# The rank of what feeds TensorE's small products, in a list scheduler's backward pass

## Chip, cores, metric

The kernel runs on one core of one Trainium2 chip. The metric is device time in microseconds (us) of one execution, as a median of several runs; lower is better.

## What is computed

64 samples `x` of 64 channels by 1024 steps go through a per-sample channel mixing (a 64x64 matrix picked by a condition index) and then, for each of the 4096 rows, a feed-forward layer of 1024 to 1024 with a gated low-rank part (8 experts of rank 16, two of them chosen per row). The input is added at the end:

```python
y = einsum('bct,bcd->bdt', x, weights[condition])
logits = einsum('bsd,ed->bse', y, gate_w)             # 8 experts
w, sel = top_k(logits, 2); w = softmax(w)
w_full = sum(one_hot(sel, 8) * w[..., None], axis=2)
low = einsum('bsd,erd->ebsr', y, lora_A)
out = einsum('bsd,od->bso', y, base_w) + base_b
out = out + 2.0 * einsum('ebsr,eor,bse->bso', low, lora_B, w_full)
return x + out
```

All of it is float32.

## The kernel before

**Tiling.** The 4096 rows are 32 tiles of 128 (two samples each). Mixing channels and multiplying by the weights commute, so the kernel first forms z = x times the weights (1160 columns in three chunks: the low-rank and gate columns with the first part of the output, then two chunks of 388), and mixes the channels afterwards by a product with a 128x128 block-diagonal condition matrix. The contraction of 1024 is cut into four blocks `k` of 256, each of two halves of 128.

**Three products for one.** Every float32 operand is split into a high and a low part: ScalarE casts the high part (`copy`, recorded at L232), VectorE subtracts for the low part (`sub`, recorded at L229), and TensorE adds up high times high, low weights times high, and high weights times low. One `zstep` (line 402) is these three matmuls for one half (`f`) of one block.

**Stages.** Tiles 0 to 3 are multiplied plainly (the list `PLAIN`, 96 steps of two halves), because the weights are still arriving: `load_w` brings a weight block b(k+1)(c+1), `split_w` splits it, `load_x` and `split_x` do the same for x blocks. From tile 4 on, two tiles at a time form a pair that is multiplied with a fast 2x2-block scheme of fewer products (`p1` to `p20`), on sums of x blocks (`sum_x`, L290) and sums of weight blocks (`mix_w`, L340), with results put together by ScalarE and VectorE (L710, L727).

**Small products.** For every tile, z is split again (`split_z`) and multiplied with the condition matrix (`sums`, line 428). For chunk 0 this gives the gate's logits; `gate` chooses and weighs the experts in small steps on ScalarE and VectorE, `tr` transposes the weighted low-rank part on TensorE, and `sums` with `with_lora` adds its product. These products (`sums` and `tr`) are short next to the stream of z products. `add` is called with `first=True` for them in tiles 0 to 29. `finish` closes a chunk, `store` writes the tile.

**The condition matrix** of a tile comes by `load_cond` (line 386): GpSimd issues an indirect gather into `bdr`, ScalarE casts it to `bdh` (L392's first `add`, recorded at L232), VectorE subtracts to `bdl` (L229). There are two buffers of each, so tiles 0 and 2 share one. The gather is a step with `early=True`.

**The order of the work** is made by a planner. The kernel's functions don't emit instructions; they call `add` on a `Program`, which records a step: its engine (or engines), a cost, what it reads and writes, a due time, and some marks. `run` (line 109) then does two passes:

- a backward pass gives each step a rank `late`: the latest start by which everything that depends on it is still in time, by the steps' costs, the time `hop` for a signal between engines, and `lag` for a transfer;
- a forward pass simulates the engines with these costs. For the engine that is free first, it takes among the steps that are ready the one with the smallest `(not first, late)`, and emits it. A step is ready when all that it depends on has ended, by the planner's own costs; a step with `early` is moreover not offered before `late - AHEAD` (10 us); a `first` step is offered MARGIN (1.2 us) after its inputs are ready, and then goes ahead of all steps that are not `first`.

The emitted order is the order of each engine's queue. Every engine works through its queue in that order, and an instruction whose input hasn't arrived holds up those behind it. The z products have the extra key `"order"`, so among themselves they keep the written order. Planner costs that matter here: ScalarE's `START` 0.74, GpSimd's 1.7, `FLIGHT` 2.0 and 1/360e3 us per byte for a transfer.

SP issues the loads of x (L274), weights (L324), tokens (L375) and `in_lb` (L589); GpSimd issues the gathers (L389), the accumulating loads (L376, L383) and the stores (L458). Eight semaphores are used in turn for SP's transfers, so a transfer also waits for the one eight places before it to land.

Of the kernel before, what the change touches and what calls it, by code (L numbers as in the profile page):

```python
# [52 lines left out]
MARGIN = 1.2  # L53
# [24 lines left out]
class Program:  # L78
# [30 lines left out]
    def run(self):  # L109
        steps, n = self.steps, len(self.steps)  # L110
        succ = [[] for _ in steps]
        for i, s in enumerate(steps):
            for d in s["deps"]:
                succ[d].append(i)
        hop = lambda a, b: SAME[a] if a == b else HOP[a]
        late = [0.0] * n
        for i in reversed(range(n)):
            s = steps[i]
            c, e = min(s["eng"].values()), next(iter(s["eng"]))
            late[i] = min([s["due"] - c] + [late[j] - hop(e, next(iter(steps[j]["eng"]))) - s["lag"] - c  # L120
                                            for j in succ[i]])
        left = [len(s["deps"]) for s in steps]
        ready, end, by = [0.0] * n, [0.0] * n, [None] * n
        free = dict(START)
        cand = {e: set() for e in HOP}

        def offer(i):
            for e in steps[i]["eng"]:
                t = max([steps[i]["after"]] + [end[d] + hop(by[d], e) for d in steps[i]["deps"]])
                if steps[i]["early"]:  # L130
                    t = max(t, late[i] - AHEAD)
                t += MARGIN if steps[i]["first"] else 0.0
                cand[e].add((i, t))

        for i in range(n):
            if not left[i]:
                offer(i)
        done, port, wire = 0, 0.0, 0.0
        while done < n:
            best = None  # L140
            for e, c in cand.items():
                if c:
                    t = max(free[e], min(max(r, port) if steps[i]["port"] else r for i, r in c))
                    if best is None or t < best[0]:
                        best = (t, e)
            t, e = best
            i, r = min(((i, r) for i, r in cand[e] if (max(r, port) if steps[i]["port"] else r) <= t + 1e-9),
                       key=lambda q: (not steps[q[0]]["first"], late[q[0]], q[0]))
            for f in steps[i]["eng"]:
                cand[f] = {q for q in cand[f] if q[0] != i}  # L150
            end[i], by[i] = t + steps[i]["eng"][e], e
            free[e] = end[i]
            if steps[i]["size"]:
                end[i] = wire = max(end[i] + FLIGHT, wire) + steps[i]["size"] * DMA
            if steps[i]["port"]:
                port = end[i]
            steps[i]["fn"](e)
            done += 1
            for j in succ[i]:
                left[j] -= 1  # L160
                if not left[j]:
                    offer(j)
        return max(end)
# [686 lines left out]
```

## Time and profile before

| | |
|---|---|
| median of 3 runs | 460.23 us (459.87 to 460.57) |
| the profiled execution | 460.46 us, of which span 458.7 us |
| granted TensorE clock | 1.00 of full speed over the span |
| bytes from and to HBM | 57.74 MB read, 16.78 MB written |

The profile is of one execution. Its span goes from the first to the last instruction; the execution's own time holds some 1.8 us more around it. PE is TensorE's matmuls and PEld its weight loads, DVE is VectorE, ACT ScalarE, POOL GpSimd, SP the engine that issues most loads. Lines are those of the kernel's file; since ScalarE's casts and VectorE's subtractions go through helpers, they all carry L232 and L229, and are told apart by the names of their tiles (out<-in). In a timeline a row has its start and duration in us, then engine, line, operation, tiles and shapes; the brackets at its end give the time that the engine stood idle just before it, and what ended that. The ends of matmuls are modelled: back to back they start 0.176 us apart and are shown as 0.34 long.

### The profile page before, as it was taken

How to read it: one execution, taken by the hardware profiler on the slowest of the kernel's cores; microseconds unless marked ns; L12 is line 12 of the kernel's file. 1: busy time of each engine (PE TensorE's matmuls, PEld its weight loads, DVE VectorE, ACT ScalarE, POOL GpSimd, SP SyncE). 2: the span in 40 equal slices, each digit the busy share in tenths (PEclk: the TensorE clock that was granted, in tenths of full speed). 3: DMA queues.
4: the chain of work that ended last, by engine and by line, in shares of the span. 5: the costliest groups of instructions: out<-in, count | busy, mean ns of one | idle time of the engine just before them, and what ended most of it. 6: DMA issues, size and time to landing. Idle time of an engine off the chain costs nothing.

```text
span 458.7 us, 7562 instructions
## 1 busy us (share of the span) xinstructions
PE 452.3 (99%) x2615; PEld 449.0 (98%) x2615; DVE 383.4 (84%) x940; ACT 227.5 (50%) x520; POOL 88.8 (19%) x107
## 2 busy tenths in 40 slices
PE   8999999999999999999999999999999999999995
PEld 8999999999999999999999999999999999999995
DVE  5999997878989788796997979789797988888674
ACT  5864656543636345373543646355354544546231
POOL 3010215121303021120303003030120403103000
PEclk9999999999999999999999999999999999999999
DMA  8942739976778462764846566573655746456142
GB/s 284 336 126 42 160 98 205 214 215 198 176 211 202 172 161 88 215 128 167 188 137 189 119 185 150 172 181 110 196 120 177 182 128 195 114 176 148 48 137 91
DMA packets 36085, 75.00 MB, mean 164 GB/s; under 512 B 4416, under 2 KB 22096, under 8 KB 36048
## 3 DMA queue, kind: packets, MB, share of 16 engines
q0 software_dynamic: 10560, 36.72, 33.7%
q1 hardware_dynamic: 25200, 37.41, 26.0%
q10 hardware_dynamic: 288, 0.40, 0.3%
q8 instruction: 20, 0.33, 0.3%
q14 instruction: 17, 0.14, 0.1%
HBM read 57.74 MB, written 16.78 MB: 162 GB/s over the span
## 4 chain that ended last, share of the span: by engine, by line
PE 93%; DMA 5%; DVE 1%; SPq 1%; ACT 0%; issue 0%; ACTq 0%
PE ps_z L409 71%; PE ps_o L441 15%; PE ps_a L441 6%; DMA xtok<-in_lb 2%; DMA w_b<-in_w 2%; DMA xr<-in_xT 1%; PE ps_a L492 1%; SPq L324 0%; SPq L274 0%; DVE xtok L451 0%; DVE wl_b_b L229 0%; ACT wh_b_b L232 0%; DVE st L727 0%; ACTq L232 0%
## 5 line engine op out<-in xcount | busy, mean ns | idle before, releaser
L229 DVE TENSOR_TENSOR xl<-xr,xh 128x512 fp32r<-128x512 f32 (+1 forms) x138 | 92.3, 672 | 20.6 <-ACT xh L232 20.3
L409 PE MATMUL ps_z<-wh_t_p,xh 128*128 128x388 f32 (+1 forms) x308 | 105.3, 342 | 0.1
L409 PE MATMUL ps_z<-wl_t_p,xh 128*128 128x388 f32 (+1 forms) x308 | 104.3, 339 | 0.0
L409 PE MATMUL ps_z<-wh_t_p,xl 128*128 128x388 f32 (+1 forms) x308 | 104.3, 339 | 0.0
L232 ACT CAST xh<-xr 128x512 fp32r<-128x512 f32 (+1 forms) x136 | 82.5, 610 | 37.4 <-PE ps_z L409 32.8
L727 DVE TENSOR_TENSOR st<-ps_z,st 128x388 f32<-128x388 f32 x126 | 70.3, 559 | 21.0 <-PE ps_z L409 19.9
L290 DVE TENSOR_TENSOR xr<-xr 128x256 f32<-128x256 f32 (+1 forms) x139 | 69.7, 528 | 3.1 <-DMA xr<-in_xT 2.7
L409 PE MATMUL ps_z<-wh_b_p,xh 128*128 128x388 f32 (+1 forms) x180 | 61.4, 341 | 0.0
L409 PE MATMUL ps_z<-wh_b_p,xl 128*128 128x388 f32 (+1 forms) x180 | 60.8, 338 | 0.0
L409 PE MATMUL ps_z<-wl_b_p,xh 128*128 128x388 f32 (+1 forms) x180 | 60.8, 338 | 0.0
L409 PEld LDWEIGHTS ps_z<-wh_t_p,xh 128*128 128x128 f32 x308 | 57.8, 188 | 1.2 <-DVE st L727 0.7
L409 PEld LDWEIGHTS ps_z<-wl_t_p,xh 128*128 128x128 f32 x308 | 57.9, 188 | 0.0
L409 PEld LDWEIGHTS ps_z<-wh_t_p,xl 128*128 128x128 f32 x308 | 57.8, 188 | 0.0
L458 POOL DMA_DIRECT2D out<-xtok x30 | 16.8, 560 | 193.5 <-DVE xtok L451 92.2
L232 ACT CAST zh<-st 128x388 fp32r<-128x388 f32 (+1 forms) x70 | 36.2, 517 | 24.2 <-DVE st L727 17.0
L376 POOL DMA_DIRECT2D xtok<-in_bias x28 | 27.4, 980 | 97.3 <-DMA xtok<-in_x 90.0
L389 POOL DMA_INDIRECT bdr<-in_cw,rows x32 | 36.1, 1129 | 28.0 <-DVE zl L229 16.6
L710 ACT ACTIVATE ps_z<-ps_z 128x388 f32<-128x388 f32 x42 | 20.1, 478 | 41.1 <-PE ps_z L409 39.0
L451 DVE TENSOR_TENSOR xtok<-ps_o,xtok 128x388 f32<-128x388 f32 x56 | 31.0, 559 | 11.0 <-PE ps_o L441 10.6
L229 DVE TENSOR_TENSOR zl<-st,zh 128x388 fp32r<-128x388 f32 (+1 forms) x70 | 38.9, 556 | 1.5 <-ACT zh L232 1.2
L409 PEld LDWEIGHTS ps_z<-wh_b_p,xh 128*128 128x128 f32 x180 | 33.8, 188 | 0.2
L409 PEld LDWEIGHTS ps_z<-wl_b_p,xh 128*128 128x128 f32 x180 | 33.8, 188 | 0.0
(130 smaller groups left out, 871.1 us busy)
## 6 DMA issues: line engine op xcount, KB each, us to landing
xr<-in_xT SPq DMA_DIRECT2D x128, 128.0 KB, 3.1
xtok<-in_bias POOLq DMA_DIRECT2D x32, 512.0 KB, 7.2
out<-xtok POOLq DMA_DIRECT2D x30, 512.0 KB, 3.1
xtok<-in_x SPq DMA_DIRECT2D x28, 512.0 KB, 3.7
w_b<-in_w SPq DMA_DIRECT2D x10, 388.0 KB, 5.8
xtok<-in_x POOLq DMA_DIRECT2D x4, 512.0 KB, 6.2
out<-xtok SPq DMA_DIRECT2D x4, 194.0 KB, 2.5
bdr<-in_cw,rows POOLq DMA_INDIRECT x32, 5.3
```

The lines of the kernel that those rows point to most:

```text
L229: eng[e].tensor_tensor(o, a, b.bitcast(F32), ALU.subtract)
L232: (nc.scalar.copy if e == ACT else nc.vector.tensor_copy)(o, a)
L290: add(DVE, tt_cost(2 * P * len(os)), lambda e: nc.vector.tensor_tensor(some(xr, os), some(xr, xs), some(xr, ys), f), [("xr", u) for u in s ...
L376: add(POOL, 1.1, lambda e: nc.gpsimd.dma_start(xtok[j], bias.broadcast_to([P, T]), accum_op=ALU.add), writes=keys, size=TWICE * 4.0 * T * P)
L389: add(POOL, 1.04, lambda e: nc.gpsimd.indirect_dma_start(out=bdr[j], out_offset=None, in_=cw, in_offset=bass.IndirectOffsetOnAxis(ap=rows[ ...
L409: nc.tensor.matmul(z, l[:, j, n], w.ap()[:, f, :cols], start=(start and q == 0), stop=(stop and q == 2), skip_group_check=True)
L441: nc.tensor.matmul(d, l, r, start=(start and m == 0), stop=(stop and m == len(mms) - 1), skip_group_check=True)
L451: add(DVE, 0.09 + 0.00104 * (s.stop - s.start), lambda e: nc.vector.tensor_tensor(xtok[j][:, o], bank[b][:, s], xtok[j][:, o], ALU.add), [ ...
L458: add(POOL, 1.0, lambda e: nc.gpsimd.dma_start(out[i * P:(i + 1) * P, o], xtok[j][:, o]), src, size=4.0 * P * (o.stop - o.start))
L492: add(PE, 0.107, lambda e: nc.tensor.matmul(tp, low[i % 2][:, :ER], ident, is_transpose=True, start=False, stop=False, skip_group_check=True),
L710: add(ACT, 0.2 + 0.00085 * W, lambda e: nc.scalar.mul(z[b], z[x], scale), [BANKS[x]], [BANKS[b]])
L727: add(DVE, 0.09 + 0.00104 * W, lambda e: nc.vector.tensor_tensor(unit(u), a(), b(), f), reads, [ukey(u)])
```

## The change

One term is added in the backward pass. Where a step's successor is marked `first`, the successor's rank is taken MARGIN (1.2 us) earlier before the step's own rank is worked out from it. MARGIN is the distance that the forward pass already keeps between the end of a small product's inputs and the time at which it is offered.

```diff
@@ -117,7 +117,7 @@
         for i in reversed(range(n)):
             s = steps[i]
             c, e = min(s["eng"].values()), next(iter(s["eng"]))
-            late[i] = min([s["due"] - c] + [late[j] - hop(e, next(iter(steps[j]["eng"]))) - s["lag"] - c
+            late[i] = min([s["due"] - c] + [late[j] - MARGIN * steps[j]["first"] - hop(e, next(iter(steps[j]["eng"]))) - s["lag"] - c
                                             for j in succ[i]])
         left = [len(s["deps"]) for s in steps]
         ready, end, by = [0.0] * n, [0.0] * n, [None] * n
```

The steps, their costs, their data and their engines stay as they are. Only `late` differs, and with it the choice in the forward pass and the time at which `early` steps are offered.

## The prediction

> **What bounds the kernel now.** I read the page first: its span, its engines, and the stretches of the span.
>
> ```profile
> span 458.7 us, 7562 instructions
> PE 452.3 (99%) x2615; PEld 449.0 (98%) x2615; DVE 383.4 (84%) x940; ACT 227.5 (50%) x520; POOL 88.8 (19%) x107
> ```
>
> TensorE (PE) is idle for 6.4 us in all. The table of busy time by stretch says where (columns: us; PE, PEld, DVE, ACT, POOL busy; clock; DMA share; GB/s):
>
> ```profile
> 0.00:20.00 20.00, 18.67 (x119) 17.78 (x120) 14.91 (x29) 13.31 (x23) 4.08 (x11) 1.00 0.92 328
> 20.00:60.00 40.00, 39.88 (x230) 39.45 (x229) 38.15 (x81) 24.36 (x53) 6.08 (x7) 1.00 0.49 116
> 100.00:430.00 330.00, 330.00 (x1904) 329.00 (x1903) 278.99 (x711) 159.07 (x374) 64.55 (x74) 1.00 0.61 164
> 453.00:459.00 6.00, 0.91 (x6) 0.58 (x4) 1.09 (x2) 0.00 (x0) 0.00 (x0) 0.95 0.35 124
> ```
>
> From 60 us on nothing is left to win: matmul follows matmul at 0.176 us. The change adds and removes no instruction, it only reorders. So it can gain the few stalls in the first 30 us and the last 20, and it can lose wherever a reordered feeder comes late. The place with little lead is the head, where each engine runs just behind the loads. So I read the timeline there, and the view of the tile `bdr` (the gathered condition weights).
>
> ```profile
> 8.21 0.40 ACT L232 CAST xh<-xr 128x256 fp32r<-128x256 f32 x1
> 9.01 0.84 ACT L232 CAST wh_b_b<-w_b 128x776 fp32r<-128x776 f32 x1 [0.40 <-DMA w_b<-in_w]
> 9.76 0.40 ACT L232 CAST xh<-xr 128x256 fp32r<-128x256 f32 x1
> 9.88 0.97 DVE L229 TENSOR_TENSOR wl_b_b<-w_b,wh_b_b 128x776 fp32r<-128x776 f32 x1 [0.24 <-ACT wh_b_b L232]
> 10.77 0.42 DVE L229 TENSOR_TENSOR xl<-xr,xh 128x256 fp32r<-128x256 f32 x1
> 11.33 0.34 PE L409 MATMUL ps_z<-wh_b_b,xh 128*128 128x384 f32 x1
> 11.51 0.34 PE L409 MATMUL ps_z<-wl_b_b,xh 128*128 128x384 f32 x1
> 11.68 0.35 PE L409 MATMUL ps_z<-wh_b_b,xl 128*128 128x384 f32 x1
> ```
>
> The cast at 9.01 is the split of weight block b22, the one at 9.76 the split of x(1,1) (tile 1, k=1). DVE subtracts behind them. The three matmuls are the first step that uses x(1,1); its last one needs `xl`, which ends at 11.19. That is a lead of 0.49 us and no more.
>
> ```profile
> 14.85 0.29 ACT L232 CAST bdh<-bdr 128x128 fp32r<-128x128 f32 x1
> 6.94 1.06 POOL L389 DMA_INDIRECT bdr<-in_cw,rows  x1 [0.18 <-issue]
> DMA to landing us min/median/max: 5.5/5.5/5.5
> ```
>
> The first gather is issued at 6.94 and lands 5.5 us later, at 12.44 (the last line is for that gather alone). Its cast waits for nothing today, because it runs at 14.85.
>
> **What the change moves, part by part.** *Rank.* Line 120 takes MARGIN (1.2) off the rank of whatever feeds a product marked `first` (5 for each of the first 30 tiles, 150 in all), and once more for every such product further down the chain. From the first cast the chain before passes 4 such products, after 20, since the PSUM banks link the tiles. Worked out with the costs in the code, ranks near the start move by 8 to 16, the last ones by 1.2. The gather is a step with `early`, offered no sooner than its rank less AHEAD: its rank goes from 16.23 to 5.34, and so it is offered at once. By the planner's own constants it is issued at 3.4 (1.7 + 1.1 + 0.6) and its cast fits at 8.5, into ScalarE's short wait for b22. So the cast of tile 0 moves from place 18 to place 10 on ScalarE, its subtraction on VectorE from 32 to 11. The built program shows it:
>
> ```
> ACT before: wh_b_b | xh | wh_b_b (b22) | xh | wh_b_p | xh | ... | xh | bdh (waits for the gather)
> ACT after:  wh_b_b | xh | bdh (waits for the gather) | wh_b_b (b22) | xh | wh_b_p | xh | bdh | ...
> ```
>
> *The wait that this adds.* GpSimd's queue and SP's first 19 transfers stand as before, and none of them up to 12.4 us waits for ScalarE, so the gather should land at 12.44 again. Queued behind the waiting cast are b22's split, x(1,1)'s, and every later weight block; VectorE waits for these, PE for both. Worked through:
> 1. Cast start: 12.44 plus 0.02 to 0.10. The upper is the weight block b23 further on (the chain has it landing at 21.51 + 3.63 = 25.14, its cast starts at 25.24); I take 0.10: 12.54.
> 2. The cast takes 0.29, and ScalarE starts the next 0.09 before the end (9.01 + 0.84 against 9.76): b22's split starts at 12.74 instead of 9.01, 3.73 late.
> 3. x(1,1)'s `xl` is late by the same and ends at 14.92. The third matmul had 0.49 of lead, 0.03 of it signalling (9.85 to 9.88). PE is late by 3.73 - 0.46 = 3.27.
>
> PE's hole comes in two pieces. From 11.33 to `xh` of x(1,1) at 10.16 + 3.73 = 13.89, 2.6 us; then two matmuls, then 0.7 for `xl`. Behind it the feeders are fast enough not to open it again: a weight block and an x block cost ScalarE 1.15 (9.01 to 9.76 plus 0.40), VectorE 1.31 at most (9.88 to 10.77 plus 0.42), with a 0.96 weight sum between some of them, and feed four steps of 0.53 = 2.1 us on PE.
>
> *What goes away.* The only other stall worth naming before the tail:
>
> ```profile
> 26.12 0.97 DVE L229 TENSOR_TENSOR wl_b_b<-w_b,wh_b_b 128x776 fp32r<-128x776 f32 x1 [0.56 <-ACT wh_b_b L232]
> 26.67 0.34 PE L409 MATMUL ps_z<-wh_b_b,xh 128*128 128x388 f32 x1
> 27.14 0.44 PE L409 MATMUL ps_z<-wl_b_b,xh 128*128 128x388 f32 x1
> 27.42 0.34 PE L409 MATMUL ps_z<-wh_b_b,xl 128*128 128x388 f32 x1
> ```
>
> b23 landed at 25.14 and its low half came late: 27.14 - 26.67 - 0.176 = 0.29, then 0.10 more, 0.40 in all. After, PE gets here at 29.9, and the load does not move by that much (it waits for a buffer that VectorE frees at about 20.9, and was issued at 21.51). ScalarE takes tile 0's `low` copy before b23's cast; the product it copies (26.15) moves up five steps of 0.53, to 26.8 after the shift, and ends near 27.5; copy 0.27, cast 0.84 and subtraction 0.97 put the low half near 29.6. The 0.40 goes.
>
> *Edits I cost at nothing.* On PE 171 of 820 steps change place, by 10 at most, small products forward. PE has no gap between 60 and 430 that these could fill, so no gain; if a small product came before its feeder, PE would stand for that feeder, 0.56 for a `zl`. That is covered by VectorE's idle 51 us of 330. SP's 52 moved transfers (4 places at most, 0.45 each) are mostly x loads that wait for a buffer anyway. The load of `in_lb` goes behind four x loads of 128 KB, 512 KB or about 1.5 us at 328 GB/s: it lands near 22.5 instead of 21.0, and its cast, now four places later on a late ScalarE, comes after that. GpSimd's 39 moves (3 places at most) put gathers before stores, and only the next token load waits for a store, for its buffer; if that came late, the closing add (0.56) and then PE's bank would be late. The last 30 us have unmarked products (tiles 30 and 31): the same.
>
> Sum against the profiled execution: 458.7 + 3.27 - 0.40 = 461.6 of span; with its own 1.8 around the span (460.46 in all) 463.3. That execution lies 0.23 above the median, so **463.1 us**, 0.6% slower.
>
> A rule that speaks against stopping there is in the Trainium skill, TensorE: Matmul & The Clock Gate, Part 1: a PE idle for one window of about 3.4 us drops to half clock, and needs a busy window to recover. By the page, a drop would add some 1.7 us (an estimate: half of one window). The hole is 2.6 + 0.7 with two matmuls between, just under the page's limit.
>
> The row: the last matmul starts at 453.57, and the clock of 453 to 459 is 0.95, which is 0.6 us at half. So PE stood for 4.6 us before the clock fell. 2.6 is well short of that, so I count no drop.
>
> **Rivals.**
> - *The clock falls in the hole.* For it: the two pieces are close together. The kernel opens with 39 matmuls over 3.94 us to raise the clock; half of such a stretch lost is 2.0: **465.1**. Chance 0.10.
> - *A second wait.* VectorE is late by 3.73, PE by 3.27, and VectorE is busy 38.15 of 40 us from 20 to 60. If b23's 0.40 stays, and the 0.46 of lead lost shows once more: 463.1 + 0.86 = **464.0**. Against it: half of ScalarE and the slots of later weights have us to spare. Chance 0.12.
> - *The gather comes sooner: not slower.* The same view over all 32 gathers reads 2.4, 5.3 and 7.4 us (least, median, most); 2.4 is also the quickest of the first four. It would land at 9.34, b22's split start at 9.64, 0.63 late, PE 0.17 late; less 0.40: 460.23 - 0.23 = **460.0**. It decides below a landing of about 9.6. Against it: DMA at 328 GB/s and a share of 0.92 in that stretch. With it stands the case that the reorder does nothing. Chance 0.06.
>
> **How the numbers follow.** The forecast has 0.72. About 0.2% (0.9 us) is what a measurement of this kernel can tell from no change. Below 461.2 lies only the last rival: same 0.04, faster 0.02 (it would need gains I cannot point at), slower 0.94. Range: a first gather as slow as the slowest, 7.4, adds 1.9 (465.0), as the clock does; a landing 1.1 sooner gives 462.0. So 462.0 to 465.1.
>
> **What would show it.** ScalarE's idle before its first `bdh`, near 3.9 us, put down to the DMA of `bdr`; `bdh` near 12.5; PE's first steps with a gap at 11.3 to 13.9 and a smaller one to 14.9; no gap at b23; from 60 on every chain piece about 2.9 later than before; the same tail. It is wrong if `bdh` stands at 9 to 10, if the stall is regained later, or if the clock row of 12 to 20 is below 1.

## The result, and the profile after

The changed kernel takes 464.86 us (median of 6 runs, 463.44 to 466.23) beside 460.21 (459.87 to 460.69) for the one before: a ratio of 1.0101 with an interval of 1.0088 to 1.0114. It is slower by about 1%, some 4.65 us. The profiled execution took 466.0 us, of which 464.1 are span, so it is one of the slower ones; before's was 460.46 with 458.7 of span. The sums below are between these two spans, 5.4 us apart.

The head of the page and the busy time by stretch (us; PE, PEld, DVE, ACT, POOL busy; clock; DMA share; GB/s), changed kernel:

```profile
span 464.1 us, 7585 instructions
PE 453.9 (98%) x2615; PEld 449.9 (97%) x2615; DVE 384.1 (83%) x940; ACT 227.5 (49%) x520; POOL 90.8 (20%) x107
```

```profile
0.00:20.00 20.00, 14.99 (x88) 13.76 (x89) 10.82 (x24) 10.52 (x21) 5.82 (x12) 0.91 0.92 327
20.00:60.00 40.00, 40.00 (x232) 39.89 (x231) 37.09 (x77) 22.37 (x49) 5.56 (x6) 1.00 0.39 93
100.00:430.00 330.00, 329.95 (x1905) 328.35 (x1904) 280.02 (x711) 159.95 (x374) 64.01 (x73) 1.00 0.60 162
```

PE's busy time in all is 1.6 us more than before with the same 2615 matmuls, and its idle time is larger as well. Both come from the first stretch: 88 matmuls in 20 us where there were 119, at a mean clock of 0.91 where there was 1.00. From 20 us on, the picture is that of before.

ScalarE's timeline, changed kernel:

```profile
8.71 0.40 ACT L232 CAST xh<-xr 128x256 fp32r<-128x256 f32 x1
13.25 0.30 ACT L232 CAST bdh<-bdr 128x128 fp32r<-128x128 f32 x1 [4.14 <-DMA bdr<-in_cw,rows]
13.46 0.83 ACT L232 CAST wh_b_b<-w_b 128x776 fp32r<-128x776 f32 x1
14.20 0.40 ACT L232 CAST xh<-xr 128x256 fp32r<-128x256 f32 x1
```

The cast of the gathered block now stands ahead of b22's split and of x(1,1)'s. ScalarE waits 4.14 us for the gather with both queued behind it; b22's split starts at 13.46, before at 9.01.

TensorE's timeline, changed kernel:

```profile
10.87 0.34 PE L409 MATMUL ps_z<-wh_b_b,xl 128*128 128x384 f32 x1
14.65 0.44 PE L409 MATMUL ps_z<-wh_b_b,xh 128*128 128x384 f32 x1 [3.44 <-ACT xh L232]
14.93 0.33 PE L409 MATMUL ps_z<-wl_b_b,xh 128*128 128x384 f32 x1
15.68 0.69 PE L409 MATMUL ps_z<-wh_b_b,xl 128*128 128x384 f32 x1 [0.41 <-DVE xl L229]
16.16 0.52 PE L409 MATMUL ps_z<-wh_b_b,xh 128*128 128x384 f32 x1
16.48 0.52 PE L409 MATMUL ps_z<-wl_b_b,xh 128*128 128x384 f32 x1
```

The matmul at 15.68 is the one that stood at 11.68 before: 4.00 us late. Behind the hole the next two start 0.32 us apart, not 0.176, and are shown 0.52 long. That is TensorE at half clock.

At b23 the stall has gone (TensorE, changed kernel; before, these three started at 26.67, 27.14 and 27.42):

```profile
29.45 0.34 PE L409 MATMUL ps_z<-wh_b_b,xh 128*128 128x388 f32 x1
29.63 0.34 PE L409 MATMUL ps_z<-wl_b_b,xh 128*128 128x388 f32 x1
29.81 0.34 PE L409 MATMUL ps_z<-wh_b_b,xl 128*128 128x388 f32 x1
```

The balance of the spans, from the distances of matmul starts over 0.176 us in the two traces: +4.00 at the hole, +1.46 from the half clock behind it (the starts from 16 to 20 us), -0.40 at b23, and +0.22 in small pieces, the largest a new wait of 0.21 and 0.10 at 421.94. That is 5.28; the last matmul starts 5.22 later than before (458.79, 453.57).

### The profile page after: what moved, and what is told of

It reads as the page before. It is cut to its first block, busy times and chain, and to the rows that moved or that the text cites. A ratio compares the mean times of both kernels' runs of the same rounds, so it can differ in the third digit from the quotient of the medians.

```text
span 464.1 us, 7585 instructions
## 1 busy us (share of the span) xinstructions
PE 453.9 (98%) x2615; PEld 449.9 (97%) x2615; DVE 384.1 (83%) x940; ACT 227.5 (49%) x520; POOL 90.8 (20%) x107
## 4 chain that ended last, share of the span: by engine, by line
PE 94%; DMA 4%; DVE 1%; issue 0%; ACT 0%; SPq 0%; ACTq 0%
PE ps_z L409 72%; PE ps_o L441 15%; PE ps_a L441 6%; DMA w_b<-in_w 2%; DMA xr<-in_xT 2%; PE ps_a L492 1%; DVE xr L290 0%; DVE xl L229 0%; DVE xtok L451 0%; DVE st L727 0%; ACT xh L232 0%; DVE zl L229 0%; SPq L324 0%; DVE l L481 0%; DVE mx L478 0%
## 5 line engine op out<-in xcount | busy, mean ns | idle before, releaser
L389 POOL DMA_INDIRECT bdr<-in_cw,rows x32 | 37.7, 1180 | 30.8 <-DVE l L481 17.8
L232 ACT CAST bdh<-bdr 128x128 fp32r<-128x128 f32 x32 | 9.6, 299 | 56.4 <-PE ps_o L441 52.3
```

Of the source, the lines that this page charges most:

```text
L232: (nc.scalar.copy if e == ACT else nc.vector.tensor_copy)(o, a)
L389: add(POOL, 1.04, lambda e: nc.gpsimd.indirect_dma_start(out=bdr[j], out_offset=None, in_=cw, in_offset=bass.IndirectOffsetOnAxis(ap=rows[ ...
```

## The experiments

Each runs beside the kernel before on the same chip, and each ratio is to that.

| kernel | median us | ratio (interval) |
|---|---|---|
| casts back behind the first weights | 460.57 | 1.0014 (1.0005 to 1.0024) |
| hoist alone, on the kernel before | 464.75 | 1.0092 (1.0075 to 1.0109) |
| hole filled with products | 463.57 | 1.0078 (1.0061 to 1.0095) |
| gather issued sooner | 463.77 | 1.0073 (1.0057 to 1.0090) |
| changed kernel again | 464.66 | 1.0095 (1.0079 to 1.0110) |
| gather issued later | 465.79 | 1.0125 (1.0109 to 1.0140) |
| b23 first, on the kernel before | 461.52 | 1.0036 (1.0024 to 1.0048) |
| casts back and b23 first | 460.22 | 1.0011 (0.9999 to 1.0023) |
| gather priced 4 us dearer | 460.61 | 1.0017 (1.0007 to 1.0027) |
| gather priced 6 us dearer | 460.73 | 1.0012 (1.0003 to 1.0021) |

### Undoing the hoist, and doing it alone

The first kernel is the changed one with the casts of the first two gathered blocks held back in the plan:

```diff
-        add(ACT, 0.28, lambda e: copy(e, bdh[j], bdr[j]), [("bdr", j)], [("bdh", j)])
+        add(ACT, 0.28, lambda e: copy(e, bdh[j], bdr[j]), [("bdr", j)], [("bdh", j)], after=14.0 if i < 2 else 0.0)
```

> The changed kernel, with the casts of the first two gathers (tiles 0 and 1) not offered before 14.0 on the planner's clock, so that they stand behind the split of x(0,3), where tile 0's stood before. All other ranks as changed. Theory (the hoisted cast alone costs the time): ScalarE no longer waits for bdr, no hole at 11 to 15 us, no fall of the clock; 459.8 to 460.5 us, since the 0.40 at b23 goes and the changed kernel's small stall of 0.3 at 422 us stays. Rival (the ranks cost something along the whole run): 463 or more.

The second is the kernel before, with only the first two gathers offered at once, so that their casts move forward and every rank stays as it was:

```diff
-            ["rows"], [("bdr", j)], size=4.0 * P * P, early=True)
+            ["rows"], [("bdr", j)], size=4.0 * P * P, early=i > 1)
```

> The kernel before, old ranks, with the mark early taken from the gathers of tiles 0 and 1 alone; by the built order tile 0's cast then stands ahead of b22's split on ScalarE, as in the changed kernel. Theory: the whole loss shows without any change of rank: 463 to 466.5 us, a hole of about 3.5 to 4.3 us at x(1,1), and a clock below 1 behind it. Rival (the loss needs the new ranks): 460.2 us.

Casts back: 460.57 us, 0.07 above the theory's range, with no wait of ScalarE for the gather. TensorE has no hole: at 11.64 it waits 0.47 in all for x(1,1)'s step, since b22's split starts at 9.41 here and not at 9.01, but it had come to that place sooner, and the step's last matmul stands at 11.64 where it was 11.68 before. Hoist alone: 464.75 us, with the changed kernel's wait in ScalarE's timeline, and behind it the third matmul of x(1,1)'s step in TensorE's:

```profile
12.54 0.30 ACT L232 CAST bdh<-bdr 128x128 fp32r<-128x128 f32 x1 [4.16 <-DMA bdr<-in_cw,rows]
```

```profile
14.97 0.60 PE L409 MATMUL ps_z<-wh_b_b,xl 128*128 128x384 f32 x1 [0.42 <-DVE xl L229]
```

The profiled execution took 465.76 us, the longest of this kernel's four. TensorE's step is 3.29 late in it and the half clock behind it takes some 1.6 more, less b23's 0.40. Another 1.1 lie in three waits between 252 and 261 us that neither the kernel before nor the changed one has in its profile. (VectorE waits 1.72 us for an x load at 256.06, between the first and the second; that this makes the later two was not shown.) Whether the other three runs had these waits is not known. With that reserve, the hoisted cast alone makes nearly the whole loss, and all the other reordering together costs about 0.6 us (ratio 1.0014; by its interval 0.2 to 1.1). TensorE's timeline of the kernel with the casts back shows where most of it lies:

```profile
26.19 0.34 PE L409 MATMUL ps_z<-wh_b_b,xh 128*128 128x388 f32 x1
27.08 0.44 PE L409 MATMUL ps_z<-wl_b_b,xh 128*128 128x388 f32 x1 [0.55 <-DVE wl_b_b L229]
27.36 0.34 PE L409 MATMUL ps_z<-wh_b_b,xl 128*128 128x388 f32 x1
```

This is b23's stall, 0.81 where it was 0.40 before (the distances of starts over 0.176). Tile 0's small product (three matmuls, 0.53 us) stands ahead of b23's step in the kernel before and fills part of the wait; here it stands behind it. So the 0.40 did not go here, as the theory had it. Another 0.31 is a wait at 417.37, for the same product as the changed kernel's at 421.94.

### Filling the hole

44 products of zeros into a bank that is not in use stand ahead of x(1,1)'s first step. They keep TensorE at work and shorten no wait of ScalarE:

```diff
+            if key == ("plain", 1, 0, 1, 0):
+                for _ in range(44):
+                    nc.tensor.matmul(bank["o1"][:, :P], wz, wz, start=True, stop=True)
```

> The changed kernel, with 44 small matmuls on zeros (the warm-up's, into a bank not yet in use) ahead of the first step of x(1,1), where TensorE stands and waits. They add work and take no wait away. Theory: the clock stays at 1.00 from 5 us on, and 1.7 of the loss goes: 464.9 - 1.7 = 463.2 us. Rival (the slow clock costs nothing, since TensorE would wait for its feeders there anyway): 464.9 us or a little more.

463.57 us, about 1.1 us (the difference of the two ratios, 0.0023 of 460) under the changed kernel, or 0.8 under its second series. The intervals of these ratios overlap, so the times alone do not give the size; the trace and the clock do. The busy time by stretch of this kernel:

```profile
11.51:14.93 3.42, 2.70 (x40) 2.20 (x37) 1.44 (x3) 2.22 (x5) 0.95 (x1) 1.00 1.06 388
14.93:18.34 3.41, 3.21 (x18) 3.21 (x19) 3.41 (x7) 3.41 (x8) 0.00 (x0) 1.00 1.02 379
```

The clock stays at 1.00 (all four runs have a mean clock of 0.999 or more) and the 16 to 20 us excess is 0.02 instead of 1.46. The wait for the data stays (cast at 12.71, the third matmul of x(1,1)'s step 3.45 late), so the time does not go back to before's. Wait and clock are two losses that add.

### Moving the gather

Sooner: the identity matrix, built by GpSimd ahead of the gathers, is built behind the first two.

```diff
+        def gather(e):
+            nc.gpsimd.indirect_dma_start(
...
+            if i == 1:
+                make_identity(nc, ident)
...
-    add(POOL, 0.6, lambda e: make_identity(nc, ident), writes=["ident"])
```

> The changed kernel, with the identity matrix built on GpSimd behind the first two gathers and not ahead of them: the gather is issued 0.7 to 1.1 us sooner, ScalarE's order near it stays. Theory (TensorE's hole follows the gather's landing one to one): the landing and bdh come 0.7 to 1.1 sooner, the hole is shorter by the same: 464.0 us if the clock still falls, 462.3 if the shorter hole keeps it. Rival (the DMA engines are full, and an earlier issue lands no earlier): 464.9 us.

Later: GpSimd first fills a 128x1024 tile that is not yet in use. The changed kernel runs beside it once more.

```diff
-    add(POOL, 0.6, lambda e: make_identity(nc, ident), writes=["ident"])
+    add(POOL, 0.6, lambda e: (make_identity(nc, ident), nc.gpsimd.memset(xtok[1], 0.0)), writes=["ident"])
```

> The changed kernel once more, beside the next one on the same chip. Both theories: 464 to 465 us, the first gathered block cast on ScalarE near 13.2 us, the clock at half for about 3.4 us from 15.3.

> The changed kernel with a 128x1024 fill on GpSimd ahead of its gathers, so that the first is issued about 1 us later than 7.39. Theory 1 (the landing follows the issue, and the time follows the landing): the first cast of a gathered block comes about 1 us later than 13.25, TensorE's first hole is 1 us longer, 465.5 to 466 us. Theory 2 (the landing is set by what else is in the DMA queues at 12 to 13 us, and hardly by the issue): the cast stays within 0.4 us of 13.25 and the time within 0.4 us of the changed kernel's, 464.5 to 465.2 us.

ScalarE's timeline of the later gather, and then of the changed kernel beside it:

```profile
13.10 0.30 ACT L232 CAST bdh<-bdr 128x128 fp32r<-128x128 f32 x1 [4.49 <-DMA bdr<-in_cw,rows]
```

```profile
12.39 0.30 ACT L232 CAST bdh<-bdr 128x128 fp32r<-128x128 f32 x1 [3.70 <-DMA bdr<-in_cw,rows]
```

In this second profile of the changed kernel the gather was issued at 6.68, in the first at 7.39, in the kernel with GpSimd's fill at 7.47. Beside the second profile GpSimd's fill put the issue 0.79 and the cast 0.71 back, and the median time rose by 1.1 (the two profiled executions can't be compared by their times, 465.56 and 465.84, for the reason given below). The cast lies within 0.4 us of 13.25, as theory 2 had it, but only because the first profile's gather was a late one; landing and time moved with the issue, as theory 1 had it, though the 1.1 is more than the 0.71, and that difference is not explained. One trace of each is thin evidence: in the eight traces with an issue between 6.48 and 6.68 the gather's last completion lies anywhere from 11.91 to 12.69. The two late issues, 7.39 and 7.47, gave 13.23 and 13.07. The sooner kernel does not do the opposite: issued at 6.04, the block was cast only at 12.70, 6.66 us later, no sooner than where the gather was issued at 6.6 (the hoist alone, 12.54). The packet records and the semaphore's updates in the traces show at which point the sooner kernel lost its lead. The gather's first packet moves 4.22 us after the issue here and 4.25 in the hoist alone, and the first of its 16 completions comes 0.54 sooner (11.02, 11.56). But the last of the 16, which the cast waits for, comes at 12.68, in the hoist alone at 12.52: thirteen are in by 11.90, and the other three come at 12.34, 12.39 and 12.68. Why these three were slow is not shown. The kernel's four runs took 462.9 to 465.06 us, two at a mean clock of 0.999 and two at 0.995 and 0.996, and its ratio's interval overlaps that of the changed kernel.

The second profile of the changed kernel has one more thing to show. TensorE's timeline on both sides of the hole, and busy time by stretch:

```profile
10.98 0.34 PE L409 MATMUL ps_z<-wh_b_b,xl 128*128 128x384 f32 x1
13.78 0.69 PE L409 MATMUL ps_z<-wh_b_b,xh 128*128 128x384 f32 x1 [2.47 <-ACT xh L232]
14.81 0.69 PE L409 MATMUL ps_z<-wh_b_b,xl 128*128 128x384 f32 x1
```

```profile
9.92:13.33 3.41, 1.40 (x8) 1.08 (x7) 0.29 (x1) 0.94 (x2) 0.05 (x1) 1.00 1.06 391
13.33:16.74 3.41, 2.93 (x8) 2.43 (x9) 3.29 (x5) 3.41 (x9) 0.90 (x1) 0.50 1.03 394
16.74:20.16 3.42, 3.42 (x13) 3.42 (x12) 3.42 (x6) 2.57 (x6) 0.00 (x0) 0.50 1.06 375
20.16:23.57 3.41, 3.41 (x21) 3.41 (x20) 3.41 (x6) 1.88 (x3) 0.00 (x0) 1.00 0.97 327
```

The hole is shorter here (TensorE's largest idle piece is 2.47 us, from 11.31), yet the clock falls 2.0 us after TensorE stopped, and stays at half for 6.83 us, twice as long as in the first profile. The excess from 15 to 20.5 us is 2.5. The two executions took 466.0 and 465.84 us, for different reasons.

### b23's load

What is left of before's stalls is b23. The kernel before with that load issued ahead of others:

```diff
-            size=8.0 * P * P)
+            size=8.0 * P * P, after=17.3 if 2 <= i < 4 else 0.0)
...
-    add(SP, ISSUE, lambda e: nc.sync.dma_start(xtok[2], lb), writes=lraw, size=4.0 * T * P)
+    add(SP, ISSUE, lambda e: nc.sync.dma_start(xtok[2], lb), writes=lraw, size=4.0 * T * P, after=17.3)
```

> The kernel before, with the load of weight block b23 issued ahead of the x loads of tiles 2 and 3 and of the load of in_lb. Theory 1 (the 0.40 us stall of the kernel before at 26.67 to 27.42 is b23's load alone): the load lands 2 to 3 us sooner than 25.14, the stall is gone, nothing else moves, 459.7 to 459.9 us, a ratio near 0.999. Theory 2 (what is put behind it, x of tiles 2 and 3 or in_lb, comes late instead): a new stall of 0.4 us or more between 17 and 30 us, 460.2 us or more.

The same two edits on the changed kernel with its casts back:

> The changed kernel with its first two casts of gathered blocks put back behind the first weights, and b23's load moved as in the run before. Theory 1 (the 0.5 us that is left when the casts alone are put back is the stall at b23): 459.7 to 460.1 us. Theory 2 (it is the late p15 product near 418 us and others spread out): 460.3 to 460.7 us.

In both the stall at b23 is gone, and neither beats the kernel before. On the kernel before it costs 1.5 us (461.52), though neither theory had the place. VectorE's timeline first, then TensorE's:

```profile
79.14 0.69 DVE L290 TENSOR_TENSOR xr<-xr 128x512 f32<-128x512 f32 x1 [2.49 <-DMA xr<-in_xT]
```

```profile
81.53 0.45 PE L409 MATMUL ps_z<-wh_t_p,xh 128*128 128x388 f32 x1 [0.29 <-ACT ps_z L710]
...
84.32 0.44 PE L409 MATMUL ps_z<-wh_t_p,xh 128*128 128x384 f32 x1 [0.40 <-DVE st L727]
```

An x load lands late at 79 us (the loads of that stretch take 5.5 us from issue to landing in the median, 3.7 in the kernel before), and TensorE stands twice for what follows from it: 1.2 us (0.45 and 0.11, 0.55 and 0.11 over the usual distance). GpSimd's accumulating loads stand in another order in this plan; that these hold the load up was not shown. With the casts back as well there is no such wait; 460.22 us lies between the ranges of the two theories and can't be told from the kernel before. A wait of 0.34 and 0.11 near 416 us stands where b23's 0.40 is gone, so theory 2 has a part in it too.

### Telling the planner when the gather lands

The forward pass, which decides when a cast is offered, counts on a gather's data by its `FLIGHT` and its bytes. (The backward pass allows a transfer 3.0 us more, `QUEUE`; the forward pass does not.) Two kernels keep the new term and add a fixed time to the landing of every gather in both passes, 4 us in the first, 6 us in the second. The gathers' own ranks move by it too:

```diff
-                               lag=FLIGHT + QUEUE + size * DMA if size else 0.0, after=after,
+                               lag=FLIGHT + QUEUE + size * DMA + slow if size else 0.0, after=after, slow=slow,
...
-                end[i] = wire = max(end[i] + FLIGHT, wire) + steps[i]["size"] * DMA
+                end[i] = wire = max(end[i] + FLIGHT, wire) + steps[i]["size"] * DMA; end[i] += steps[i]["slow"]
...
-            ["rows"], [("bdr", j)], size=4.0 * P * P, early=True)
+            ["rows"], [("bdr", j)], size=4.0 * P * P, early=True, slow=4.0)
```

> The changed kernel, with 4 us more on the planner's landing time of every gather. The first cast of a gathered block goes from place 10 of ScalarE's order to place 12, still ahead of its data: in the trace of before the cast ahead of it there ends at 11.7, the gather lands at 12.4 to 13.2. Theory 1 (a wait costs only what lead TensorE lacks behind it): ScalarE waits 0.7 to 1.5 us, the weight block queued behind it is first needed by TensorE near 14.5 and has more than 1 us of lead, so there is no hole, the clock stays full, 460.0 to 460.8 us. Theory 2 (any wait of ScalarE for the gather passes to TensorE whole): 460.8 to 461.6 us.

> The changed kernel, with 6 us more on the planner's landing time of every gather; the first cast is then at place 16 of ScalarE's order, as in the kernel before. Theory 1 (the loss is the planner's too early landing time of the gather, and the new rank does no harm apart from it): no wait, no hole, 459.8 to 460.6 us. Theory 2 (the new rank costs by itself, in the 30 tiles of the middle): 460.8 us or more, with stalls of TensorE between 60 and 430 us.

460.61 and 460.73 us. With 4 us ScalarE still waits for the gather (its timeline):

```profile
12.47 0.30 ACT L232 CAST bdh<-bdr 128x128 fp32r<-128x128 f32 x1 [0.69 <-DMA bdr<-in_cw,rows]
```

TensorE has no hole there, 0.15 us of excess from 10.5 to 16 us: the block queued behind that cast is needed late enough. With 6 us the cast stands at before's place and there is no wait; the median lies 0.13 above what theory 1 gave, with stalls of 0.55 at b23 and 0.37 near 417 us and none above 0.11 between 60 and 410. (Counted as in the prediction, from the rows of ScalarE's timeline, the cast stands at place 14 with 4 us and at 18 with 6, not 12 and 16.) So by itself the new rank gains nothing here; it costs about 0.6 us (ratio 1.0012; by its interval 0.1 to 1.0). The large cost is that it reaches a step whose landing time the plan has wrong.

## Why the prediction came out as it did

**The mechanism held.** It was the hoisted cast, waiting for the gather with b22's and x(1,1)'s splits behind it; the prediction put the loss there, and the two kernels that undo and isolate the hoist show it. The time lies 1.76 us above the 463.1 predicted: in its sum, one term was mis-sized and one was left at nothing. It is nearer to the 465.1 of the rival with 0.10. That it is inside the range is luck for the sum: the upper end was put there for a gather as slow as the slowest (1.9 us) or a fall of the clock (2.0 us), each alone, and it holds a smaller delay of the gather together with a fall of the clock. One of the signs that the prediction named for being wrong also came, a clock row of 12 to 20 us below 1: it is 0.79 in the changed kernel.

**The landing (12.44, cast at 12.54).** In the first profile the cast started at 13.25. GpSimd's queue stood as before in order but ran later: the gather was issued at 7.39 instead of 6.94, and was in flight for 5.8 instead of 5.5 us. GpSimd's timeline and the view of the tile, changed kernel:

```profile
7.39 1.17 POOL L389 DMA_INDIRECT bdr<-in_cw,rows  x1 [0.18 <-issue]
```

```profile
DMA to landing us min/median/max: 5.8/5.8/5.8
```

**The chain from the cast to TensorE (3.27 late).** It held closely. The late cast adds 0.71 to the 3.27, which gives 3.98; the trace has 4.00. In the hoist alone the cast came at the predicted 12.54, and the step is 3.29 late. In the second profile, where the cast came at 12.39, the third matmul of x(1,1)'s step starts at 14.81, 3.13 after before's 11.68.

**"I count no drop" is the step that failed.** The prediction read from before's tail that TensorE stood for 4.6 us before the clock fell, and called 2.6 well short of that. By the clock's record it is 4.5 us, from 453.91, where the last matmul is shown to end, to 458.39. The 2.6 was too short for the first profile: the first piece of its hole is 3.60 (14.65 - 10.87 - 0.176), since the cast came 0.71 later and TensorE had come there 0.29 sooner. But length was not what decided: the second profile has 2.62 (13.78 - 10.98 - 0.176), as forecast, and the clock fell all the same. The tail cut at the clock's own steps (busy time by stretch, kernel before):

```profile
451.56:454.97 3.41, 2.35 (x14) 2.02 (x13) 2.41 (x6) 0.00 (x0) 0.00 (x0) 1.00 0.58 205
454.97:458.38 3.41, 0.00 (x0) 0.00 (x0) 0.00 (x0) 0.00 (x0) 0.00 (x0) 1.00 0.29 103
```

and the hole of the changed kernel cut likewise:

```profile
8.45:11.86 3.41, 2.76 (x16) 2.30 (x14) 1.35 (x2) 0.67 (x2) 1.10 (x2) 1.00 1.06 411
11.86:15.27 3.41, 0.61 (x2) 0.30 (x2) 1.24 (x3) 2.02 (x5) 0.95 (x1) 1.00 1.04 378
15.27:18.69 3.42, 3.01 (x9) 3.01 (x10) 3.42 (x7) 3.42 (x9) 0.00 (x0) 0.50 1.04 382
18.69:22.10 3.41, 3.41 (x21) 3.41 (x21) 3.41 (x6) 2.56 (x5) 0.00 (x0) 1.00 0.97 334
```

The clock changes only at the ends of such stretches of 3.41 us: in the clock records of the twelve traces, every length between two changes is a whole number of them (1, 2, 3, 130, 132, 133 or 134). In the tail, the stretch in which the last matmul ended was busy for 2.35 us of 3.41 and did not count; the fall came at the end of the second one. The 4.5 us were thus the rest of one stretch and the whole of the next, not a length that an idle time needs. From the last matmul's end to the fall it was 4.1 us in the first profile and 2.0 in the second. In the hole, 0.61 us of work within the stretch did not prevent the fall. The cost is 1.46 in this profile, between nothing, which the forecast took, and the 2.0 of the rival that had 0.10; in the second profile, with two stretches at half clock, it is about 2.5.

The rule that the prediction set aside is in the Trainium skill, TensorE: Matmul & The Clock Gate, Part 1. The estimate of 1.7 us that the prediction worked out from it lies near the 1.46, not near the 2.5. The same section says that the window is 3413 ns long and "free-running". From this one can work out that it does not start with the idle time. The traces agree: half clock for 3.41 us (15.27 to 18.69) and 6.83 us (13.33 to 20.16), the fall at a different place each time.

Where the clock stayed up, the forecast's time came out. The kernel whose hole was filled, with the clock at 0.999 or more in every run, took 463.57 us. One run in six of the changed kernel had a mean clock of 0.998, and it took 463.44 us; the others had 0.992 to 0.996 and 464.56 to 466.23. Of the hoist alone and of the sooner gather, the three runs at 0.998 or more took 463.56, 462.9 and 463.33. These runs have no trace, so that the clock did not fall in their hole is inferred from that mean.

**b23's 0.40** went, as worked out. **The edits costed at nothing** were worth +0.22 in the profile, and the casts-back kernel puts them at about 0.6 with b23's stall included. **The second wait** (0.12) did not show: PE is busy 40.00 of 40 us from 20 to 60. **The gather sooner** (0.06) never came near its limit of 9.6: in the seven profiles in which a cast waited for it, that cast began at 12.39 to 13.25.

## What to carry to other kernels

A planner's rank does harm where it can reach a step whose time it has wrong: before a rank is made more urgent, compare the plan's landing times with the trace, above all for transfers at the start, and ask what is queued behind the first step that gets moved. In an engine that works in order, the price of such a wait is the lead of what stands behind it: 4.14 us at place 10 of ScalarE's order cost TensorE 4.00, 0.69 us at place 14 cost it no more than 0.15. And price a hole in TensorE's work twice, for the wait and for the clock, by how empty it leaves a stretch of 3.41 us wherever that stretch may begin, not by its longest idle piece.

## What the runs showed of the hardware

**How much work keeps the clock.** Cutting the traces at the clock's steps, stretches of 3.41 us in which TensorE was busy for 0.07 (gather later), 0.61 (changed kernel), 0.72 (gather sooner), 0.74 (hoist alone) and 1.40 us (changed kernel again) were followed by half clock; stretches with 1.71 and 2.70 (hole filled, tail and head) and 2.35 us (kernel before, tail) were not. The ends of matmuls are modelled, so these are rough, and what lies between 1.40 and 1.71 is open. So is why one fall lasted two stretches and the others one; the first stretch at half clock was busy for 2.93 us where a second followed (13.33 to 16.74), and for 3.01 where none did (15.27 to 18.69).

**A gather under load.** The first gather, 64 KB, landed 5.4 to 6.6 us after its issue in the twelve traces, with the DMA engines at a share of 1.04 to 1.06 and 387 to 393 GB/s from 8 to 15 us; the quickest of all 32 in the kernel before took 2.4. Of this time, 4.0 to 4.3 us pass in every trace before its first packet moves; the rest, 1.2 to 2.4 us, is until the slowest of its 16 completions. The fit in the Trainium skill, DMA: Bandwidth & Descriptors, Anatomy of one DMA — SWDGE (gpsimd) path, gives some 2.15 us for these bytes (an estimate, 2.0 plus 65,536 over 436,000). The measured 2.4 of the quickest gather lies near it; the 5.4 to 6.6 of the first one do not. Why the first packet waits 4 us, and which of the 16 comes last, was not settled.
